# The normalization step of each layer norm: nine ScalarE instructions, or four two-scalar VectorE instructions

## The chip, the cores and the metric

The kernel runs on one core of a Trainium2 chip. The metric is the device time of one launch in microseconds (us). The core's engines each run their own queue of instructions in order: PE (TensorE, matmuls), DVE (VectorE), ACT (ScalarE), POOL (GpSimd) and SP (SyncE, which issues most DMAs). Weight loads of PE are shown apart, as PEld.

## The reference, cut to what matters

An input of 4 images of 64 x 64 positions with 128 channels passes through four layers, all in float32.

```python
def _ln(x, w, b):
    mu = x.mean(-1, keepdims=True)
    var = ((x - mu) ** 2).mean(-1, keepdims=True)
    return (x - mu) * jax.lax.rsqrt(var + 1e-05) * w + b
...
# layer 0, a state space layer
xz = _ln(input, ln1_w, ln1_b) @ in_proj_w            # ln1
...                                                  # 3x3 depthwise conv, silu
def step(h, t):                                      # 4 directions, 256 channels x 16 states, 4096 steps
    h = jnp.exp(d_t[..., None] * A) * h + (d_t * x_t)[..., None] * B_t[:, :, None, :]
    return (h, jnp.einsum('bkdn,bkn->bkd', h, C_t))
...
x = input + y @ out_proj_w
h2 = jax.nn.gelu(_ln(x, ln2_w, ln2_b) @ fc1_w + fc1_b, approximate=False) @ fc2_w + fc2_b   # ln2
x = x + h2
# layer 1: attention over all 4096 positions, layer 2: a block of convolutions
# layer 3: 7x7 neighborhood attention, then an MLP
x = x + _neighborhood_attention(_layernorm(x, norm1_g, norm1_b), ...)   # norm1
y = jax.nn.gelu(_layernorm(x, norm2_g, norm2_b) @ fc1_w + fc1_b, approximate=False)   # norm2
return x + y @ fc2_w + fc2_b
```

Four layer norms over 128 channels matter here: ln1, ln2, norm1 and norm2. Each is done in chunks of 512 positions, 8 chunks to an image, so there are 4 x 4 x 8 = 128 calls.

## The kernel before, in words

**The stages.** For each image: `scan_inputs` (ln1, projections, the 3x3 convolution, the step sizes), `selective_scan` (the recurrence), `scan_output` (gating, output projection, ln2, MLP), `layer1`, `layer2`, `layer3_attention` (norm1) and `layer3_mlp` (norm2, MLP). The scan is the long work of DVE and POOL, and the other stages are laid beside it. While image 0 is scanned, `scan_inputs` of images 1 to 3 is done. While image n is scanned, the rest of image n - 1 is done, with the last MLP of image n - 2 joined to its `scan_output`. When the last scan is over, the rest of image 3 follows alone, with the MLP of image 2 at its start and that of image 3 at its end.

**The scan.** It works in 512 units for each image; a unit is two tiles of 128 rows x 512 steps. POOL multiplies `dB` for both (L501, 128x1024, four buffers). For each of the two, ACT makes `dA = exp(...)` into one of three PSUM buffers (L507), and DVE runs the recurrence (L509) with `dA` from PSUM and `dB` from SBUF. For most units DVE writes the result over `dA` and then multiplies it by the row of C into `hc` (L514). For 5 of 16 units in image 0, and 7 of 16 in the others, DVE writes the states to `hc` and POOL multiplies (L522); that instruction is issued two units later. ACT copies the last state (L516, L518). PE sums the products (L555).

**A layer norm** (`layernorm_T`) takes four groups of 128 positions. DVE makes mean and variance (L188, L190), ACT makes `rstd = exp(-0.5 ln(var + eps))` (L174, L175). The step that is changed writes `xn`, of which there is one buffer. PE transposes the four groups into PSUM (L201), and ACT applies the weight and the bias (L202). In what follows "a call" is one such chunk.

**The order.** No order is written out by hand. The kernel names priorities (the scan has a late one, so that the other stages go first where they can), and a scheduler, which works with its own estimates of how long each instruction takes, lays out each engine's queue before the kernel runs. Dependencies between engines become semaphores. Groups of Gelu and of Silu are held together on ACT, because they need another table than Exp and Ln; each such group loads a table before and after it (L96, L226, L359).

A second path, `everything_again`, is in the program for inputs whose values are out of bounds. It also calls `layernorm_T`, but it isn't run with these inputs.

Other lines that are spoken of: L598 and L601 scale and set up weights on DVE at the start of each `scan_output`. L889, on POOL, takes a power in the setup of layer 2, and L890 to L894 are DVE instructions beside it. L1100, L1101, L1151 and L1198 to L1205 are small DVE instructions that check bounds or set up a bias table. L328 is POOL's product `du` in `scan_inputs`. L623 and L648 are gating and sum on DVE in `scan_output`.

Of the kernel before, what the change touches and what calls it, by code (L numbers as in the profile page):

```python
# [28 lines left out]
F32 = mybir.dt.float32  # L29
AF = mybir.ActivationFunctionType  # L30
ALU = mybir.AluOpType
# [140 lines left out]
def rstd_of(nc, K, out, var):  # L172

    nc.scalar.activation(out, var, AF.Ln, bias=K.eps)  # L174
    nc.scalar.activation(out, out, AF.Exp, scale=-0.5)  # L175


def layernorm_T(tc, K, pool, psum, x, w, b, out):


    nc = tc.nc
    stats = pool.tile([128, 4, 6], F32, name="ln_stats", bufs=2)
    mv = pool.tile([128, 4, 2], F32, name="ln_mv", bufs=2)
    rstd = pool.tile([128, 4], F32, name="ln_rstd", bufs=2)
    less = pool.tile([128, 4], F32, name="ln_less", bufs=2)
    shift = pool.tile([128, 4], F32, name="ln_shift", bufs=2)
    for t in range(4):
        nc.vector.bn_stats(stats[:, t, :], x[:, t, :])  # L188
    for t in range(4):
        nc.vector.bn_aggr(mv[:, t, :], stats[:, t, :])  # L190
    rstd_of(nc, K, rstd, mv[:, :, 1])
    nc.scalar.activation(less, rstd, AF.Copy, scale=-1.0)
    for t in range(4):
        nc.scalar.activation(shift[:, t : t + 1], mv[:, t, 0:1], AF.Copy, scale=less[:, t : t + 1])
    xn = pool.tile([128, 4, 128], F32, name="ln_xn", bufs=1)
    pt = psum.tile([128, 4, 128], F32, name="ps")
    for t in range(4):
        nc.scalar.activation(  # L198
            xn[:, t, :], x[:, t, :], AF.Identity, bias=shift[:, t : t + 1], scale=rstd[:, t : t + 1]
        )  # L200
        nc.tensor.transpose(pt[:, t, :], xn[:, t, :], K.ident)  # L201
    nc.scalar.activation(out, pt.rearrange("p t c -> p (t c)"), AF.Identity, bias=b, scale=w)  # L202
# [74 lines left out]
def scan_inputs(tc, K, A, D, img):  # L277
# [5 lines left out]
    with ExitStack() as ctx:  # L283
# [50 lines left out]
        for c in range(NCH + 1):  # L334
            acts = []
            if c < NCH:
                xt = pool.tile([128, 4, 128], F32, name="x")
                nc.sync.dma_start(xt, token_tiles(A["x"][img], c))
                xnT = pool.tile([128, LC], F32, name="xnT")
                layernorm_T(tc, K, pool, psum, xt, ln_w, ln_b, xnT)  # L340
                band = pool.tile([128, ND, RC + 2, W], F32, name="band", bufs=3)
                bands[c] = band
                for d in range(ND):
                    ps = psum.tile([128, LC], F32, name="ps")
                    nc.tensor.matmul(ps, in_proj[:, d * 128 : (d + 1) * 128], xnT, start=True, stop=True)
                    rows = ps.rearrange("p (h w) -> p h w", w=W)
                    nc.scalar.copy(band[:, d, 1 : RC + 1, :], rows)
                    if c > 0:
                        nc.scalar.copy(bands[c - 1][:, d, RC + 1, :], rows[:, 0, :])
                        nc.scalar.copy(band[:, d, 0, :], bands[c - 1][:, d, RC, :])  # L350
                sz = pool.tile([128, ND, LC], F32, name="sz")
                for d in range(ND):
                    ps = psum.tile([128, LC], F32, name="ps")
                    mm = nc.tensor.matmul(
                        ps, in_proj[:, DI + d * 128 : DI + (d + 1) * 128], xnT, start=True, stop=True
                    )
                    if d == 0:
                        together.open(mm)
                    acts.append(lambda d=d, ps=ps, sz=sz: nc.scalar.activation(sz[:, d, :], ps, AF.Silu))  # L359
# [221 lines left out]
def scan_output(tc, K, A, D, img, xT, last, scan_over=None):  # L581
# [6 lines left out]
    with ExitStack() as ctx:  # L588
# [17 lines left out]
        def chunk(c, psum=psum, together=together):  # L606
# [44 lines left out]
            yield  # L651
            xnT = pool.tile([128, LC], F32, name="xnT")
            layernorm_T(tc, K, pool, psum, x, ln_w, ln_b, xnT)
            yield
            po = yield from mlp(tc, K, P, pool, psum, together, xnT, x)
# [582 lines left out]
def layer3_attention(tc, K, A, D, img, wide):  # L1238
# [7 lines left out]
    with ExitStack() as ctx:  # L1246
# [33 lines left out]
        def make_chunk(c):  # L1280
            x = pool.tile([128, 4, 128], F32, name="x", bufs=6 if wide else 2)
            nc.sync.dma_start(x, token_tiles(D.x4[img], c))
            xs[c] = x
            xn = pool.tile([128, LC], F32, name="xnT", bufs=1)
            layernorm_T(tc, K, pool, made_in, x, n_w, n_b, xn)
            ps = fresh((128, 2, LC))
            for i in range(2):
                nc.tensor.matmul(ps[:, i, :], qkv[:, span(i, C)], xn, start=True, stop=True)
            qs[c] = pool.tile([128, LC], F32, name="q")
            nc.scalar.activation(qs[c], ps[:, 0, :], AF.Identity, bias=qb, scale=HD**-0.5)  # L1290
            ks[c] = pool.tile([128, LC], F32, name="k", bufs=3)
            nc.scalar.activation(ks[c], ps[:, 1, :], AF.Identity, bias=qkv_b[:, 1:2])
            ps = fresh((128, 4, 128))
            for t in range(4):
                nc.tensor.matmul(ps[:, t, :], xn[:, span(t, 128)], qkv[:, 2 * C :], start=True, stop=True)
            vs[c] = pool.tile([128, 4, 128], F32, name="v", bufs=3)
            nc.scalar.copy(vs[c], ps)
# [477 lines left out]
```

## Time and profile before

| | |
|---|---|
| Runs of the kernel | 8887.86, 8895.40, 8905.56 us; median 8895.4 us |
| The profiled execution | 8915.71 us, span 8914.0 us, mean granted PE clock 0.866 |
| Busy in the span | PE 80%, DVE 80%, ACT 63%, POOL 79%, PEld 30% |
| Instructions | PE 30116, DVE 8483, ACT 11581, POOL 3064 |
| DMA | 1581.91 MB, mean 177 GB/s |

A page of the profile lists busy time by engine, the span in 40 slices, the DMA queues, the chain of work that ended last, and groups of instructions. A group's row reads: line, engine, operation, output <- inputs, shapes, count | busy us and mean ns of one | idle time of the engine just before these instructions, and what ended it. The timeline gives start and duration in us of single instructions.

The layer norm's other instructions on DVE are short: L188 had a median of 278 ns, L190 of 158 ns. L198 had a median of 482 ns, L194 of 280 ns and L192 of 205 ns. Short instructions that follow each other on ACT overlap a little, so that busy time is less than count times mean.

### The profile page before, as it was taken

How to read it: one execution, taken by the hardware profiler on the slowest of the kernel's cores; microseconds unless marked ns; L12 is line 12 of the kernel's file. 1: busy time of each engine (PE TensorE's matmuls, PEld its weight loads, DVE VectorE, ACT ScalarE, POOL GpSimd, SP SyncE). 2: the span in 40 equal slices, each digit the busy share in tenths (PEclk: the TensorE clock that was granted, in tenths of full speed). 3: DMA queues.
4: the chain of work that ended last, by engine and by line, in shares of the span. 5: the costliest groups of instructions: out<-in, count | busy, mean ns of one | idle time of the engine just before them, and what ended most of it. 6: DMA issues, size and time to landing. Idle time of an engine off the chain costs nothing. (4 is left out here: it accounts for less than half of the span.)

```text
span 8914.0 us, 101143 instructions
## 1 busy us (share of the span) xinstructions
PE 7120.9 (80%) x30116; PEld 2708.4 (30%) x30116; DVE 7132.4 (80%) x8483; ACT 5640.4 (63%) x11581; POOL 7043.5 (79%) x3064
## 2 busy tenths in 40 slices
PE   5844858687689898887798888777888987888987
PEld 2211313132332233333332233233322332353333
DVE  3888878888899999998899989998999989513433
ACT  5646667676566666666766666667766666454355
POOL 5987899989799998998899989988899989500000
PEclk8856968687799998898899998888899988899989
DMA  5777677777555556665555556565445566320020
GB/s 172 248 236 240 224 249 240 262 242 265 180 175 166 172 174 211 192 215 190 165 174 168 176 183 213 194 213 178 165 165 174 180 204 198 107 69 4 7 80 29
DMA packets 864124, 1581.91 MB, mean 177 GB/s; under 512 B 219701, under 2 KB 344780, under 8 KB 859213
## 3 DMA queue, kind: packets, MB, share of 16 engines
q1 hardware_dynamic: 733261, 1399.17, 47.9%
q10 hardware_dynamic: 130304, 176.19, 5.6%
q8 instruction: 241, 3.95, 0.2%
q14 instruction: 318, 2.61, 0.1%
HBM read 1280.47 MB, written 283.59 MB: 175 GB/s over the span
## 5 line engine op out<-in xcount | busy, mean ns | idle before, releaser
L501 POOL TENSOR_TENSOR dB<-du,b_rows 128x1024 f32<-128x1024 f32 x2048 | 4817.8, 2389 | 553.6 <-DVE hc L509 137.0
L507 ACT ACTIVATE dA<-dt,w_A_log 128x512 f32<-128x512 f32 x4096 | 2785.3, 690 | 487.8 <-DVE hc L509 210.9
L509 DVE TENSOR_TENSOR_SCAN dA<-dA,state,dB 128x512 f32<-128x512 f32 x2128 | 2634.8, 1275 | 242.6 <-POOL dB L501 129.4
L522 POOL TENSOR_TENSOR hc<-hc,c_rows 128x1024 f32<-128x1024 f32 x832 | 1988.6, 2390 | 34.7 <-issue 16.1
L509 DVE TENSOR_TENSOR_SCAN hc<-dA,state,dB 128x512 f32<-128x512 f32 x1456 | 1805.4, 1270 | 218.8 <-ACT dA L507 134.6
L514 DVE TENSOR_TENSOR hc<-dA,c_rows 128x512 f32<-128x512 f32 x2432 | 1568.2, 679 | 76.1 <-PE py L555 61.1
L555 PE MATMUL py<-hc,pick 128*32 128x512 f32 x8192 | 1244.2, 685 | 380.2 <-POOL hc L522 307.3
L516 ACT COPY state<-dA 128x1 f32<-128x1 f32 x2128 | 327.6, 158 | 1348.3 <-DVE hc L514 1339.5
L845 PE MATMUL pa<-e,l_v 128*128 128x512 f32 x2048 | 1069.7, 654 | 21.1 <-ACT e L801 19.9
L797 PE MATMUL pair<-l_g,l_f 32*128 32x512 f32 x2048 | 527.1, 663 | 181.1 <-ACT e L801 139.2
L801 ACT ACTIVATE e<-pair 128x1024 f32<-128x1024 f32 (+1 forms) x448 | 508.2, 1134 | 226.9 <-PE pair L797 219.1
L845 PEld LDWEIGHTS pa<-e,l_v 128*128 128x128 f32 x2048 | 375.5, 200 | 673.9 <-issue 618.1
L555 PEld LDWEIGHTS py<-hc,pick 128*32 128x32 f32 x8192 | 211.5, 116 | 1147.5 <-issue 466.4
L247 PE MATMUL ps<-band,w_conv_diag 128*128 128x504 f32 (+3 forms) x1152 | 502.1, 595 | 7.7 <-ACT delta L397 6.6
L1303 PE MATMUL pair<-table,ident 128*128 128x512 f32 x768 | 398.9, 644 | 97.2 <-ACT e L1313 76.5
L509 DVE TENSOR_TENSOR_SCAN dA<-dA,dB 128x512 f32<-128x512 f32 x304 | 356.8, 1215 | 75.6 <-POOL dB L501 62.3
L328 POOL TENSOR_TENSOR du<-delta,xc 128x1024 f32<-128x1024 f32 x128 | 334.7, 2623 | 57.2 <-ACT delta L397 48.9
L1313 ACT ACTIVATE e<-pair 128x1024 f32<-128x1024 f32 (+1 forms) x224 | 254.7, 1137 | 186.5 <-PE pair L1307 185.9
L201 PE MATMUL ps<-ident,ln_xn 128*128 128x128 f32 x512 | 136.5, 362 | 291.0 <-ACT ln_xn L198 221.6
L219 PE MATMUL ps<-xnT,w_fc_w 128*128 128x512 f32 x512 | 271.6, 666 | 71.6 <-ACT xnT L202 44.6
L247 PEld LDWEIGHTS ps<-band,w_conv_diag 128*128 128x128 f32 x1152 | 221.3, 194 | 288.7 <-issue 259.3
L797 PEld LDWEIGHTS pair<-l_g,l_f 32*128 32x128 f32 x2048 | 139.0, 188 | 537.6 <-ACT e L801 275.0
(274 smaller groups left out, 8551.0 us busy)
## 6 DMA issues: line engine op xcount, KB each, us to landing
b_rows<-bc_dram SPq DMA_DIRECT2D x1024, 256.0 KB
c_rows<-bc_dram SPq DMA_DIRECT2D x1024, 256.0 KB
dt<-delta_dram SPq DMA_DIRECT2D x512, 512.0 KB
du<-du_dram SPq DMA_DIRECT2D x512, 512.0 KB
delta_dram<-delta ACTq DMA_DIRECT2D x128, 512.0 KB
du_dram<-du SPq DMA_DIRECT2D x128, 512.0 KB
table<-biasT_dram SPq DMA_DIRECT2D x72, 512.0 KB
y_first_dram<-y_sum ACTq DMA_DIRECT2D x128, 256.0 KB
```

Source lines behind the costliest of these rows:

```text
L247: mm = nc.tensor.matmul(out[:, r0 - row0 : r1 - row0, c0:c1], lhsT((dy + 1) * 3 + dx + 1), src[:, r0 + dy : r1 + dy, c0 + dx : c1 + dx], s ...
L328: nc.gpsimd.tensor_mul(du.rearrange("p d (a b) -> p d a b", b=H), deltas[b].rearrange("p d (a b) -> p d a b", b=H), tk,)
L501: nc.gpsimd.tensor_mul(dB, dus[pp], mid(bt, 2))
L507: nc.scalar.activation(dA, dts[pp][:, g, :], AF.Exp, scale=S.A[:, k, j, pr, g : g + 1])
L509: nc.vector.tensor_tensor_scan(hg[:, order], dA[:, order], dB[:, g, order], 0.0 if i == 0 else state[:, j, pr, g : g + 1], ALU.mult, ALU.add,)
L514: mm = nc.vector.tensor_mul(hc[:, g, :], dA, ct)
L522: made.append(nc.gpsimd.tensor_mul(hc, hc, mid(ct, 2)))
L555: mm = nc.tensor.matmul(py[0][32 * q : 32 * q + 32, :], S.pick, hcs[q // 2][:, q % 2, :], start=(k == 1 and j == 0), stop=(j == NJS - 1),)
L797: nc.tensor.matmul(ps[:, u, :], f[quad, t // 4, span(t % 4, 128)], g[quad, c, :], start=True, stop=True)
L801: made = nc.scalar.activation(e, ps, AF.Exp)
L845: nc.tensor.matmul(pa, v[:, 8 * q + t, :], es[q], start=(t == 0 and q == 0), stop=(t == 7 and q == 3),)
L1303: nc.tensor.matmul(ps[:, u, :], K.ident, t[:, u, :], start=True, stop=False)
```

## The change

The two small tiles `less` and `shift` go. Before, ACT made `less = -rstd` (one instruction), `shift = mean * less` (four) and `xn = x * rstd + shift` (four). Now DVE makes `xn = (x - mean) * rstd` in four instructions, which take the mean and rstd of each position as two column scalars.

```diff
-    less = pool.tile([128, 4], F32, name="ln_less", bufs=2)
-    shift = pool.tile([128, 4], F32, name="ln_shift", bufs=2)
...
     rstd_of(nc, K, rstd, mv[:, :, 1])
-    nc.scalar.activation(less, rstd, AF.Copy, scale=-1.0)
-    for t in range(4):
-        nc.scalar.activation(shift[:, t : t + 1], mv[:, t, 0:1], AF.Copy, scale=less[:, t : t + 1])
     xn = pool.tile([128, 4, 128], F32, name="ln_xn", bufs=1)
     pt = psum.tile([128, 4, 128], F32, name="ps")
     for t in range(4):
-        nc.scalar.activation(
-            xn[:, t, :], x[:, t, :], AF.Identity, bias=shift[:, t : t + 1], scale=rstd[:, t : t + 1]
+        nc.vector.tensor_scalar(
+            xn[:, t, :], x[:, t, :], mv[:, t, 0:1], rstd[:, t : t + 1], ALU.subtract, ALU.mult
         )
         nc.tensor.transpose(pt[:, t, :], xn[:, t, :], K.ident)
     nc.scalar.activation(out, pt.rearrange("p t c -> p (t c)"), AF.Identity, bias=b, scale=w)
```

## The prediction

> **What bounds the kernel now.** I read the slices of the page first, then busy time by stretch, then single instructions in the timeline.
>
> The slices (busy tenths of each engine in 40 slices of 223 us) show two parts. Up to slice 34, about 7680 us, VectorE and POOL are both nearly full; after that POOL has nothing to do. ScalarE is never full.
>
> ```profile
> DVE  3888878888899999998899989998999989513433
> ACT  5646667676566666666766666667766666454355
> POOL 5987899989799998998899989988899989500000
> ```
>
> The same by stretch (from:to, length, then busy time and count of PE, weight loads, DVE, ACT, POOL): the layer norms before the scan (780 to 960 is one of three such stretches), the first layer norm of layer 3 beside the scan (3400 to 3920), those ahead of the two MLPs beside the scan (4050 to 4420).
>
> ```profile
> 780.00:960.00 180.00, 134.38 (x424) 51.28 (x424) 148.66 (x209) 135.56 (x338) 144.17 (x63) 0.87 0.64 217
> 3400.00:3920.00 520.00, 416.94 (x2268) 156.59 (x2272) 495.24 (x573) 343.96 (x741) 513.98 (x223) 0.87 0.65 209
> 4050.00:4420.00 370.00, 288.40 (x1173) 145.15 (x1174) 316.40 (x463) 279.64 (x647) 300.32 (x130) 0.84 0.55 183
> ```
>
> In the second POOL is busy 514 of 520 us: it is the bound, DVE (0.95) only a little behind. In the others POOL (0.80, 0.81) and DVE (0.83, 0.86) both have gaps, made by waits on each other, on ScalarE and on PE.
>
> The chain of waits breaks off in the scan, so it is of use only for the end: from 7820 us on it is mostly PE, with ScalarE's layer norm steps between.
>
> **What goes.** Groups by form (count, then busy us and mean ns):
>
> ```profile
> L198 ACT ACTIVATE ln_xn<-x,ln_shift,ln_rstd 128x128 f32<-128x128 f32 x512 | 214.4, 485 | 0.0
> L194 ACT ACTIVATE ln_shift<-ln_mv,ln_less 128x1 f32<-128x1 f32 x512 | 108.1, 284 | 1.6
> L192 ACT ACTIVATE ln_less<-ln_rstd 128x4 f32<-128x4 f32 x128 | 24.4, 201 | 2.2 <-ACT ln_rstd L175 0.5 <-ACT state L516 0.2
> L598 DVE TENSOR_SCALAR out_proj_b<-w_out_proj_w,w_onorm_b 128x128 f32<-128x128 f32 x8 | 4.9, 653 | 4.5 <-DMA w_out_proj_w<-in_L_conv_out_proj_w 4.5
> ```
>
> There are 128 layer norms. ScalarE loses 214.4 + 108.1 + 24.4 = 346.9 us, 2.71 us for each. By the starts of L192, 8 of them lie before 600 us, 24 between 780 and 1950 (image 0's scan), 23 in the layer 3 stretches and 40 in the MLP stretches beside the later scans, and 33 after 7680.
>
> **What comes.** Four DVE instructions each, 128x128 f32 from SBUF to SBUF, with two column scalars. The nearest row is L598: same shape, one column. L894 with two constants took 226 ns, L648 with a PSUM source 345; between these the cost is bounded. Two undisturbed L598 took 0.48 us together (4034.01 below), so I take 0.24 each, 0.96 a call, 123 us in all. In the order of the changed kernel the four stand in a row in nearly every case, among the scan's instructions.
>
> **The wait that comes with them.** L598 has a mean of 653 ns though its median is 284. The timeline says why (start, duration, engine, instruction). POOL:
>
> ```profile
> 2253.14 4.63 POOL L501 TENSOR_TENSOR dB<-du,b_rows 128x1024 f32<-128x1024 f32 x2
> 2257.73 2.33 POOL L522 TENSOR_TENSOR hc<-hc,c_rows 128x1024 f32<-128x1024 f32 x1
> 2260.03 4.64 POOL L501 TENSOR_TENSOR dB<-du,b_rows 128x1024 f32<-128x1024 f32 x2
> 2264.63 2.34 POOL L522 TENSOR_TENSOR hc<-hc,c_rows 128x1024 f32<-128x1024 f32 x1
> ...
> 5935.68 2.35 POOL L501 TENSOR_TENSOR dB<-du,b_rows 128x1024 f32<-128x1024 f32 x1 [2.67 <-DMA sz<-sz_dram]
> ```
>
> and DVE in the same stretches:
>
> ```profile
> 2253.60 13.52 DVE L601 TENSOR_TENSOR center<-center,ident 128x128 f32<-128x128 f32 x1
> 4034.01 0.48 DVE L598 TENSOR_SCALAR out_proj_b<-w_out_proj_w,w_onorm_b 128x128 f32<-128x128 f32 x2 [2.13 <-DMA w_out_proj_w<-in_L_conv_out_proj_w]
> 5936.63 1.67 DVE L598 TENSOR_SCALAR out_proj_b<-w_out_proj_w,w_onorm_b 128x128 f32<-128x128 f32 x2
> ```
>
> L601 lasts 13.52 us and ends at 2267.12, 0.15 us after the sixth POOL instruction in an unbroken row (2264.63 + 2.34 = 2266.97). With POOL idle (4031.6) it took 0.28. L598 at 5936.63 took 1.48 us for its first, which ends 0.08 us after POOL's L501; its second took 0.27. So a DVE instruction that reads two SBUF tensors, or is a 128x128 SBUF-to-SBUF tensor_scalar, stands still while POOL works, and is let in only when POOL pauses. The scan's own DVE instructions, which have one source in PSUM, and bn_stats (254 to 302 ns in all 512) show nothing of this. The new instruction has L598's shape, so I take it to wait too.
>
> [...]
>
> How long would each wait be? At each start of L192 beside the scan I followed POOL's queue and asked what it could still do if DVE stood still: a dB for at most four units (bufs=4), and a product only of a unit already scanned. Summed: 86 us for the 24 calls before 1950, 132 us for the 23 of layer 3, 58 us for the 40 ahead of MLPs: 276 us for 87 calls, 3.2 each. Bounds for one: 0 (not held up) and 13.52.
>
> Behind the standing instruction are queued the scans (L509) and products (L514). For them wait ScalarE's L516 and L507 (three dA buffers), then POOL, which finds no free dB. What this costs goes by stretch.
>
> - **Start (8 calls): 0.** POOL's L889, a power, lasts 20.82 us (20.74 to 41.56). If it shuts DVE out, the first eight instructions end near 44 instead of 29; it may not, for two tiny DVE instructions (L891, L892) passed beside it in 0.15 us. The first xnT (L202) waits for the load of ln_w until 48.11 anyway. Without that cover it would be some 15 us.
> - **Layer 3 (23 calls): +80.** POOL is the bound, so only POOL's idle time counts. DVE gets in when POOL has run out of free dB. POOL then idles through the four instructions (0.96) and two scans of 1.27 (2.55) until a dB comes free: 3.5 us a call. DVE cannot make the wait good before the next call (75 us × 0.05 spare = 3.7 us against 132/23 = 5.7 + 0.96), so it repeats. Bounds: 0, and the full 6.7 × 23 = 154.
> - **Before the scan's end of image 0 (24 calls): +42.** POOL has a share of 0.80 to 0.88 here, so some idle time is free. I take half of 3.5. Bounds: −31 (DVE's 10.4 us of waits for dA in the first stretch, times three, all gone) and 86 + 23 = 109.
> - **Ahead of MLPs (40 calls): 0.** Lost: up to 1.45 + 0.96 = 2.4 us a call, 96 in all. Gained: ScalarE is free of 2.71 us a call, and DVE waits there for ScalarE's dA 46.7, 35.2 and 13.1 us in the three stretches, 95 in all. I take half of each. Bounds −95 and +96.
> - **After the scan (33 calls): −20.** POOL is idle, no wait. On the chain of waits, L192, L194 and L198 stand for 22 us (four pieces of 1.7 to 2.8 in the MLP pair, 9.0 together; nine of 0.7 to 1.8 around layer 3, 9.8; 3.5 in the last MLP). Little comes back, since DVE is idle. Bounds −45 and 0.
> - **A new dependence: 0.** DVE now waits for ScalarE's rstd. Nearest rows: L623 waited 71.7 us for ScalarE in 64, 1.1 each; L648, which follows an rstd too, 5.1 us in 128. Such a wait runs into the same POOL idle time. Bounds: 0 and 87 × 1.1 = 96.
>
> The kernel's order is made by a scheduler, and POOL's and SP's instructions move by a few places too. I put nothing on this.
>
> **Sum.** 0 + 80 + 42 + 0 − 20 = +102 us. The profiled execution took 8915.7 us (span 8914.0), 20.3 above the median of 8895.4. So 8895.4 + 102 = 8997.
>
> **Rivals.**
> 1. *Faster: ScalarE's relief wins.* The standing falls into gaps that DVE has anyway (DVE idles 718 us of the 7010 in the stretches from 600 to 7660), and the MLP stretches gain: −95 × 0.6 there, −20 at the end, +20 in layer 3: 8895 − 57 = 8838. For it: DVE and POOL are both under 0.9 in 64 of the 87 calls' stretches. Against it: POOL's 0.99 in layer 3.
> 2. *The wait does not come at all*, because the form with two columns, unlike L598, runs beside POOL. Then DVE's 87 × 0.96 = 84 us hide in its gaps but for about 25, relief is as above: −57 − 20 − 31 × 0.5 + 25 = 8828. Against it: L598 and L1199 (7.28 us), both tensor_scalar.
> 3. *Far slower: every wait counts in full*, since DVE stands and nothing takes it up: 276 + 84 − 20 = +340, 9235. It decides if waits are as long as the ten I found on DVE instructions with two SBUF operands or of tensor_scalar (1.3 to 13.5 us, mean 4.6), and POOL's lead doesn't shrink. Against it: POOL works on while DVE stands.
>
> **How the numbers follow.** Forecast 0.63, rival 1 0.22, rival 2 0.06, rival 3 0.09. About 0.2% (18 us) is what a measurement of this kernel can tell from no change. The forecast's low end and rival 1's high end give 0.11 within it. Slower: 0.56 of the forecast and 0.09 of rival 3, 0.65; faster 0.24. All bounds together reach from 8724 to 9350; ends at once are unlikely. From 8850 to 9170 leaves out rival 3's upper part (0.08) and the lower parts of rivals 1 and 2 (0.12).
>
> **What would show it.** The new DVE row should have a minimum near 0.24 to 0.3 us, and beside the scan about one in four of 1 to 10 us, ending just after a POOL instruction; after the scan none. Its busy time should be near 350 to 400 us, against 123 unhindered. ScalarE should be 347 us shorter. In 3400 to 4000 POOL's share should fall below 0.97, with dB waiting for scans; after the scan the rest should be some 20 us shorter. I am wrong if the row's longest is under 0.5 us, if POOL's share in layer 3 stays, or if the MLP stretches shorten by more than 40 us.

## The result, and the profile after

| | before | after |
|---|---|---|
| Runs beside each other, median | 8891.63 us (8886.56 to 8905.56, 4 runs) | 9035.4 us (9025.69 to 9045.01, 4 runs) |
| Ratio | | 1.0155, 95% interval 1.0143 to 1.0167 |
| Profiled execution, span | 8914.0 us | 9035.4 us |
| DVE, ACT, POOL busy in the span | 80%, 63%, 79% | 84%, 59%, 78% |
| Mean granted PE clock | 0.866 | 0.855 |

The change costs 138 us by the ratio (127 to 149 by the interval; the two medians lie 144 apart); +102 was forecast. Lines of after are five below those of before from the dB product on: the new instruction is L193, dB is L496, the recurrence L504, the products L509 (DVE) and L517 (POOL).

The slices of after, each 226 us long (DVE, ACT and POOL busy, in tenths):

```profile
DVE  4888888797899999999999989999999899953433
ACT  4645656666466665565666655556666665554344
POOL 5887898978889997997799979987899899930000
```

POOL's work now ends in the 36th digit (a 3) and not in the 35th; the digits ahead of it differ by a tenth here and there, so the loss has to be read from stretches. The three stretches that the prediction showed, at their new times (from:to, length, then busy time and count of PE, weight loads, DVE, ACT, POOL; granted clock, DMA share, GB/s):

```profile
780.00:970.00 190.00, 137.28 (x408) 51.49 (x408) 167.64 (x230) 112.88 (x259) 139.60 (x61) 0.79 0.58 197
3480.00:4000.00 520.00, 399.30 (x2152) 151.24 (x2152) 502.15 (x563) 300.26 (x617) 480.62 (x208) 0.83 0.58 191
4110.00:4480.00 370.00, 280.85 (x1142) 145.12 (x1141) 343.47 (x511) 224.69 (x446) 273.04 (x118) 0.82 0.52 169
```

In layer 3 POOL is busy 480.6 of 520 us (0.92), where it was 514 (0.99): what was the bound now has gaps, while DVE, with 502, looks fuller. That fullness is not work. It is the new instruction, whose group by form is

```profile
L193 DVE TENSOR_SCALAR ln_xn<-x,ln_mv,ln_rstd 128x128 f32<-128x128 f32 x512 | 464.3, 966 | 86.8 <-PE ps L196 66.1 <-ACT ln_rstd L175 20.7
```

a mean of 966 ns. By minimum, median and longest (with first and last start), for all 512, and then for those that start after the scan:

```profile
L193 DVE TENSOR_SCALAR ln_xn<-x,ln_mv,ln_rstd x512: 302/340/7567, 23.5 to 9005.5; 128x128 f32<-128x128 f32 x171
```

```profile
L193 DVE TENSOR_SCALAR ln_xn<-x,ln_mv,ln_rstd x124: 334/341/348, 7991.1 to 9005.5; 128x128 f32<-128x128 f32 x124
```

Unhindered one took 0.34 us, and after the scan, where POOL is idle, none of the 124 took more than 0.348. Four in a row overlapped: each started 0.26 us after the one ahead of it, and a whole call took 1.11 us.

```profile
8017.22 1.11 DVE L193 TENSOR_SCALAR ln_xn<-x,ln_mv,ln_rstd 128x128 f32<-128x128 f32 x4 [3.84 <-PE ps L196]
```

Beside the scan 142 of the 512 took over 0.5 us; what they took above 0.34 adds up to 322 us, and all 142 ended 79 to 90 ns after the end of a POOL instruction.

One layer norm in layer 3, in the timeline (start, duration, engine, instruction). POOL first, then DVE:

```profile
3659.66 2.38 POOL L517 TENSOR_TENSOR hc<-hc,c_rows 128x1024 f32<-128x1024 f32 x1
3661.96 4.67 POOL L496 TENSOR_TENSOR dB<-du,b_rows 128x1024 f32<-128x1024 f32 x2
3666.55 2.38 POOL L517 TENSOR_TENSOR hc<-hc,c_rows 128x1024 f32<-128x1024 f32 x1
```

```profile
3661.45 8.34 DVE L193 TENSOR_SCALAR ln_xn<-x,ln_mv,ln_rstd 128x128 f32<-128x128 f32 x4
```

The four stand for 8.34 us. POOL goes through an unbroken row until 3668.93, and the first of the four ends just after that, at about 3669.0 (it is the one of 7.57 us); the other three then take 0.33 each. This is the picture of L601 in the profile before. Ahead of it, in `scan_inputs`, the picture is another one:

```profile
258.60 2.35 POOL L517 TENSOR_TENSOR hc<-hc,c_rows 128x1024 f32<-128x1024 f32 x1
260.91 2.36 POOL L496 TENSOR_TENSOR dB<-du,b_rows 128x1024 f32<-128x1024 f32 x1
263.22 4.64 POOL L323 TENSOR_TENSOR du<-delta,xc 128x1024 f32<-128x1024 f32 x2
```

```profile
260.44 7.50 DVE L193 TENSOR_SCALAR ln_xn<-x,ln_mv,ln_rstd 128x128 f32<-128x128 f32 x4
```

Here the four took 0.595, 2.391, 2.378 and 2.374 us: each of the last three waited for one POOL instruction, was let in, and the next waited again, though POOL's row is as unbroken. And beside one POOL instruction there was no wait at all: L884, the power (L889 before). Two calls ran in the middle of it, unhindered. POOL, then DVE:

```profile
20.66 20.82 POOL L884 TENSOR_TENSOR w_last<-w_last,mhalf 128x128 f32<-128x128 f32 x1
```

```profile
23.54 1.12 DVE L193 TENSOR_SCALAR ln_xn<-x,ln_mv,ln_rstd 128x128 f32<-128x128 f32 x4 [0.17 <-ACT ln_rstd L175]
25.30 1.11 DVE L193 TENSOR_SCALAR ln_xn<-x,ln_mv,ln_rstd 128x128 f32<-128x128 f32 x4 [0.64 <-PE ps L196]
```

The POOL instruction whose end let a held one in was a product of 128x1024 in all 142 cases (L496 71 times, L517 48, L323 23).

What the waits come to, by stage, beside what the prediction counted (87 calls by starts in the trace of before; here 88 and the first 8):

| stage | calls | instructions over 0.5 us | waited, us | longest, us | counted before |
|---|---|---|---|---|---|
| first 8 calls | 8 | 13 | 22.7 | 2.42 | not counted |
| ln1 beside scan 0 | 24 | 49 | 91.8 | 6.84 | 86 |
| layer 3 (norm1) | 24 | 27 | 116.6 | 7.57 | 132 |
| ahead of the MLPs | 40 | 51 | 87.9 | 2.45 | 58 |

Two more instructions, 3.0 us of waiting together, belong to a call of image 2's last MLP that starts at 7920.6, before the scan's end. The waits are there in about the counted size. What became of them is seen at two points of the trace, the start of the last scan instruction and that of the last sum of image 2's attention (L1342 before, L1337 after), on which the rest of image 2's layer 3 ends:

| | last scan instruction | last sum of image 2's attention | later of the two, against before | span, against before |
|---|---|---|---|---|
| before | 7699.9 | 7815.7 | 0 | 0 |
| after | 7985.3 | 7889.3 | +169.6 | +121.4 |

Before, the scan was over 116 us ahead of that attention. In those 116 us DVE and POOL had next to nothing to do:

```profile
7700.00:7816.00 116.00, 95.90 (x558) 40.28 (x556) 7.25 (x17) 28.39 (x40) 0.95 (x1) 0.90 0.15 47
```

In after it is the other way round. From 7889 to 7985 the scan runs on with little beside it, DVE is full and PE is half idle:

```profile
7889.00:7985.00 96.00, 46.73 (x180) 19.12 (x180) 94.93 (x112) 39.34 (x77) 83.38 (x37) 0.68 0.53 171
```

So the scan slipped by 285 us and the other stages by 74, and which of the two comes last has changed.

### The profile page after: what moved, and what is told of

It is laid out like the page before. It is cut to its first block, busy times and chain, and to the rows that moved or that the text cites. A ratio compares the mean times of both kernels' runs of the same rounds, so it can differ in the third digit from the quotient of the medians.

```text
span 9035.4 us, 100375 instructions
## 1 busy us (share of the span) xinstructions
PE 7148.6 (79%) x30116; PEld 2729.3 (30%) x30116; DVE 7579.7 (84%) x8995; ACT 5340.8 (59%) x10429; POOL 7048.3 (78%) x3064
## 5 line engine op out<-in xcount | busy, mean ns | idle before, releaser
L496 POOL TENSOR_TENSOR dB<-du,b_rows 128x1024 f32<-128x1024 f32 x2048 | 4806.2, 2374 | 823.4 <-DVE dA L504 195.8
L504 DVE TENSOR_TENSOR_SCAN dA<-dA,state,dB 128x512 f32<-128x512 f32 x2128 | 2627.3, 1271 | 216.4 <-POOL dB L496 109.4
L517 POOL TENSOR_TENSOR hc<-hc,c_rows 128x1024 f32<-128x1024 f32 x832 | 1976.0, 2375 | 52.4 <-issue 20.2
L504 DVE TENSOR_TENSOR_SCAN hc<-dA,state,dB 128x512 f32<-128x512 f32 x1456 | 1800.0, 1267 | 143.9 <-ACT dA L502 81.1
L509 DVE TENSOR_TENSOR hc<-dA,c_rows 128x512 f32<-128x512 f32 x2432 | 1562.0, 675 | 99.0 <-PE py L550 88.0
L193 DVE TENSOR_SCALAR ln_xn<-x,ln_mv,ln_rstd 128x128 f32<-128x128 f32 x512 | 464.3, 966 | 86.8 <-PE ps L196 66.1
L504 DVE TENSOR_TENSOR_SCAN dA<-dA,dB 128x512 f32<-128x512 f32 x304 | 356.6, 1212 | 69.4 <-POOL dB L496 50.8
L323 POOL TENSOR_TENSOR du<-delta,xc 128x1024 f32<-128x1024 f32 x128 | 332.8, 2607 | 49.8 <-ACT delta L392 43.6
```

Source lines behind the costliest of these rows:

```text
L193: nc.vector.tensor_scalar(xn[:, t, :], x[:, t, :], mv[:, t, 0:1], rstd[:, t : t + 1], ALU.subtract, ALU.mult)
L496: nc.gpsimd.tensor_mul(dB, dus[pp], mid(bt, 2))
L504: nc.vector.tensor_tensor_scan(hg[:, order], dA[:, order], dB[:, g, order], 0.0 if i == 0 else state[:, j, pr, g : g + 1], ALU.mult, ALU.add,)
L509: mm = nc.vector.tensor_mul(hc[:, g, :], dA, ct)
L517: made.append(nc.gpsimd.tensor_mul(hc, hc, mid(ct, 2)))
```

## The experiments

The intervals are at 95%, against runs of the kernel before on the same chip. Differences in us are the ratio less one, times the median of before beside it (8898 to 8903 us).

**Is it the second operand's place?** The same work in one DVE instruction of another form, with rstd as a full operand in PSUM rather than a column in SBUF. ACT writes rstd into a corner of the PSUM tile that the transposes fill afterwards, so the four transposes come after all four instructions.

```diff
-    rstd_of(nc, K, rstd, mv[:, :, 1])
+    nc.scalar.activation(rstd, mv[:, :, 1], AF.Ln, bias=K.eps)
+    nc.scalar.activation(pt[:, 3, 0:4], rstd, AF.Exp, scale=-0.5)
...
-        nc.vector.tensor_scalar(
-            xn[:, t, :], x[:, t, :], mv[:, t, 0:1], rstd[:, t : t + 1], ALU.subtract, ALU.mult
-        )
+        nc.vector.scalar_tensor_tensor(
+            xn[:, t, :], x[:, t, :], mv[:, t, 0:1], bc(pt[:, 3, t : t + 1], [128, 128]), ALU.subtract, ALU.mult
+        )
```

> The four DVE instructions become scalar_tensor_tensor with rstd read from PSUM, (x - mean) * rstd with one SBUF source, so that they are like the DVE rows that never stood still (0.33 to 0.36 us each). ScalarE is relieved as in the change, DVE has as much or more to do. If standing still beside POOL is the cause: no instruction over 0.5 us, and the time returns to before or under it, 8830 to 8900 us. If the cause is DVE's added work or the new order of instructions: 9000 to 9060 us.

Measured (e1): 8797.47 us, ratio 0.9883 (0.9866 to 0.9899), -104 us, faster than the range expected. The instruction, its group by form, and layer 3 (same columns as above):

```profile
L194 DVE SCALAR_TENSOR_TENSOR ln_xn<-x,ln_mv,ps x512: 302/341/349, 23.9 to 8769.9; 128x128 f32<-128x128 f32 x171
```

```profile
L194 DVE SCALAR_TENSOR_TENSOR ln_xn<-x,ln_mv,ps 128x128 f32<-128x128 f32 x512 | 142.2, 340 | 175.7 <-ACT ps L192 173.9 <-PE ps L198 1.5
```

```profile
3400.00:3920.00 520.00, 428.18 (x2421) 160.66 (x2420) 499.04 (x579) 326.64 (x666) 520.00 (x225) 0.88 0.63 206
```

The same 0.34 us as an unhindered L193, and not one of 512 above 0.349. POOL is busy all 520 us of layer 3. The form alone could be what differs, so the next kernel keeps the form and puts rstd back into SBUF.

```diff
-    nc.scalar.activation(pt[:, 3, 0:4], rstd, AF.Exp, scale=-0.5)
+    nc.scalar.activation(rstd, rstd, AF.Exp, scale=-0.5)
...
-            xn[:, t, :], x[:, t, :], mv[:, t, 0:1], bc(pt[:, 3, t : t + 1], [128, 128]), ALU.subtract, ALU.mult
+            xn[:, t, :], x[:, t, :], mv[:, t, 0:1], bc(rstd[:, t : t + 1], [128, 128]), ALU.subtract, ALU.mult
```

> The same scalar_tensor_tensor instructions as in the kernel with rstd in PSUM, with rstd in SBUF: two SBUF sources, nothing else. If what counts is whether an instruction stands still beside POOL: waits of 1 to 10 us come back and the time is 9000 to 9060 us. If that kernel's gain came from another thing (its transposes set after all four, the order): within 20 us of 8797.

Measured (e5): 9060.85 us, ratio 1.0179 (1.0162 to 1.0196), +159 us.

```profile
L194 DVE SCALAR_TENSOR_TENSOR ln_xn<-x,ln_mv,ln_rstd x512: 315/344/8677, 23.7 to 9026.3; 128x128 f32<-128x128 f32 x171
```

152 of them took over 0.5 us, 338 us in waits. Where four small columns lie, SBUF or PSUM, is worth 263 us of the kernel's time. With the same work on DVE and the same relief of ACT, these 338 us of waits move the last scan instruction by 290 (from 7718.8 to 8008.6).

**The wait alone, without the work.** The kernel before, with one added product of 128x2 for each layer norm, whose result nobody reads; and beside it one with a reduction of the same small size that reads one SBUF tensor.

```diff
     rstd_of(nc, K, rstd, mv[:, :, 1])
+    tiny = pool.tile([128, 2], F32, name="ln_tiny", bufs=2)
+    nc.vector.tensor_mul(tiny, rstd[:, 0:2], mv[:, 0, :])
```

> The kernel before, with one added DVE instruction per layer norm, a product of two SBUF columns of 128x2 that nobody reads (0.15 us unhindered, 19 us in all 128). If the standing beside POOL is the cause, its mean is about 3 us beside the scan and the kernel is 60 to 150 us slower than before. If not, it is within 20 us of before.

```diff
+    nc.vector.tensor_reduce(tiny, rstd.rearrange("p (a b) -> p a b", b=2), AX.X, ALU.max)
```

> The kernel before, with one added DVE instruction per layer norm at the same place as in the last one, but with one SBUF source (a maximum over pairs, 128x2 from 128x4, not read by anybody). It too waits for rstd and takes a place in DVE's queue. If standing beside POOL is the cause: never over 0.3 us, and the time within 20 us of before. If the wait for ScalarE's rstd or the place in the queue is the cause, it costs as much as the two-column product.

Measured: with the product (e2) 8992.84 us, ratio 1.0107 (1.009 to 1.0124), +95 us; with the reduction (e3) 8897.39 us, 0.9999 (0.9989 to 1.0009). First the product, then the reduction:

```profile
L193 DVE TENSOR_TENSOR ln_tiny<-ln_rstd,ln_mv x128: 116/161/9976, 24.0 to 8956.0; 128x2 f32<-128x2 f32 x128
```

```profile
L193 DVE TENSOR_REDUCE ln_tiny<-ln_rstd x128: 110/150/159, 24.5 to 8873.0; 128x2 f32<-128x4 f32 x128
```

128 instructions of 0.16 us, 20 us of work in all, cost 95 us of the kernel's time, because 47 of them were held for 147 us together. Those that read one SBUF tensor cost nothing that can be measured. Of the 78 us by which the last scan instruction came later, nearly all arose in the three layer 3 stretches (+27, +19 and +23 us, by the start of the same scan instruction in both kernels).

**After the scan alone.** Each call of `layernorm_T` is given a name, and a flag says whether the call is laid beside a scan; DVE's form is used only where a rule says so, else the code of before.

```diff
-def layernorm_T(tc, K, pool, psum, x, w, b, out):
+ON_DVE = lambda name, beside: not beside
+def layernorm_T(tc, K, pool, psum, x, w, b, out, name):
+    on_dve = ON_DVE(name, K.beside)
```

> DVE makes xn only in the layer norms of image 3's rest after the scan (and those of image 2's last MLP, 32 calls), ScalarE in all others as before. By the forecast's term for the end: 20 us faster than before, 8865 to 8885. If a shorter ScalarE does not matter at the end: 8892 within 8 us.

Measured (e4): 8869.64 us, ratio 0.9966 (0.9954 to 0.9979), -30 us, within the range of the forecast's term.

```profile
L202 DVE TENSOR_SCALAR ln_xn<-x,ln_mv,ln_rstd x128: 332/342/350, 7814.4 to 8834.9; 128x128 f32<-128x128 f32 x128
```

No wait. In its profiled execution the stretch from the end of image 2's attention to the end is 28 us shorter, 1070 us against 1098 before (and 1094 to 1100 in e6, e7 and e8 below, which change nothing there). Its span is 49 us shorter than that of before, but the other 21 us lie ahead of that point, where the code is that of before, and so is the order of instructions on DVE, ACT and POOL (on PE a few matmuls change places). They look like the spread of executions, for the profiled one of before was 12 to 24 us above its medians. The 28 us fit the -30 of the runs.

**Each stage beside the scan alone**, by the rule:

```diff
-ON_DVE = lambda name, beside: not beside
+ON_DVE = lambda name, beside: beside and name == "ln1"
```

> DVE makes xn as in the change, but only in the 32 calls of the first layer norm; ScalarE makes it in the others. By the forecast's term +42 us, 8925 to 8955. By the trace of the changed kernel, in which the rest of image 0 began 53 us later: 8930 to 8960. If waits there fall into gaps: 8895 within 20.

Measured (e6): 8985.5 us, ratio 1.0091 (1.0074 to 1.0107), +81 us, more than any of the three expectations. 62 instructions were held, for 114 us; scan 0 ended 116 us later.

```diff
+ON_DVE = lambda name, beside: beside and name == "norm1"
```

> DVE makes xn as in the change, but only in the first layer norm of layer 3 beside the scan (24 calls). By the forecast's term +80, by the kernel with the added product +67: 8950 to 8985. If only the other stretches cost: 8895 within 20.

Measured (e7): 8922.49 us, ratio 1.0025 (1.0015 to 1.0035), +22 us, a quarter of what I had put on it, and between the two expectations. The waits are there, 30 of them for 104 us, the longest longer than any in after:

```profile
L202 DVE TENSOR_SCALAR ln_xn<-x,ln_mv,ln_rstd x96: 302/335/10214, 3419.3 to 7717.7; 128x128 f32<-128x128 f32 x96
```

and the last scan instruction came 108 us later. But the attention of image 2 was done only 11 us later, and the end followed the attention. So a slip of the scan is not yet a slip of the end.

```diff
+ON_DVE = lambda name, beside: beside and name in ("ln2", "norm2")
```

> DVE makes xn as in the change, but only ahead of the MLPs beside the scan (40 calls). The forecast's term is 0: 8895 within 20. If the two to three waits of 2.4 us in each call count in full: 40 x 4 us, 9030 to 9060. If ScalarE's relief wins: under 8875.

Measured (e8): 8904.94 us, ratio 1.0005 (0.9995 to 1.0014), +4 us, no difference that can be told from none. 49 instructions held for 83 us; last scan instruction 70 us later, the attention 2 us earlier.

**Do two slips that cost little alone cost more together?** If the end waits for the later of the scan and the attention, layer 3 and MLP stages together must use up the 116 us by which the scan was ahead; if each stage has its own price, they add up to 22 + 4 = 26 us.

```diff
+ON_DVE = lambda name, beside: beside and name != "ln1"
```

> DVE makes xn as in the change in the 64 calls of layer 3 and ahead of the MLPs beside the scan, ScalarE in the rest. Each group alone moved the end of the last scan by 108 and 70 us, but the end of the kernel by 24 and 7 only: after the last scan the attention of image 2 still ran for 116 us in the kernel before, and hid the shift. If that slack is why the parts do not add up, the two together use it up: 108 + 70 - 116 = 62, 8950 to 8975. If the parts simply add: 8925 to 8935.

Measured (e9): 8973.92 us, ratio 1.0085 (1.0068 to 1.0101), +76 us. The last scan instruction is 188.5 us late, 72.7 past where the attention ended before, and the attention itself is 2 us early. The price is not a sum over stages.

**The best version.** e1's instruction beside the scans, ACT's code of before after them:

```diff
+ON_DVE = lambda name, beside: beside
...
+    if on_dve:
+        nc.scalar.activation(rstd, mv[:, :, 1], AF.Ln, bias=K.eps)
+        nc.scalar.activation(pt[:, 3, 0:4], rstd, AF.Exp, scale=-0.5)
+        for t in range(4):
+            nc.vector.scalar_tensor_tensor(
+                xn[:, t, :], x[:, t, :], mv[:, t, 0:1], bc(pt[:, 3, t : t + 1], [128, 128]), ALU.subtract, ALU.mult
+            )
```

> The instruction with rstd in PSUM, which never stood still, in the layer norms up to the end of the last scan alone; after it ScalarE makes xn as before (32 calls). If the relief of ScalarE beside the scan is worth most of the 106 us which that kernel gained: 8810 to 8840. If most of it lies after the scan: 8870 to 8900.

Measured (e10): 8784.43 us, ratio 0.9872 (0.9856 to 0.9889), -114 us, faster than either expectation. This and e1 (0.9866 to 0.9899) can't be told apart, so the relief beside the scan gives the whole of e1's gain. The scan itself ends 12 us later than before; the attention of image 2 ends 171 us earlier, so that less is left for the time after the scan.

The two points of the trace in all of these, from one profiled execution each (before had 8915.7 us, 12 to 24 above its medians, so the last column lies about that much under the differences of medians):

| | last scan instruction | last sum of image 2's attention | later of the two, against before | span, against before |
|---|---|---|---|---|
| before | 7699.9 | **7815.7** | 0 | 0 |
| after | **7985.3** | 7889.3 | +169.6 | +121.4 |
| e1, PSUM, all calls | **7718.8** | 7648.3 | -96.9 | -119.5 |
| e2, tiny product | 7777.8 | **7892.5** | +76.8 | +74.7 |
| e3, tiny reduction | 7699.2 | **7812.3** | -3.4 | -8.0 |
| e4, after the scan only | 7681.0 | **7794.6** | -21.1 | -49.1 |
| e5, SBUF, all calls | **8008.6** | 7939.2 | +192.9 | +142.1 |
| e6, ln1 only | 7777.1 | **7884.4** | +68.7 | +70.2 |
| e7, norm1 only | 7808.2 | **7827.0** | +11.3 | +6.9 |
| e8, MLPs only | 7769.8 | **7813.3** | -2.4 | -3.8 |
| e9, norm1 and MLPs | **7888.4** | 7813.6 | +72.7 | +55.1 |
| e10, PSUM, beside only | **7711.5** | 7644.3 | -104.2 | -134.9 |

The later of the two (bold) gives the span to within 5 us in every kernel where the attention is last and nothing, or the tiny instruction alone, is changed behind it (e2, e3, e6, e7, e8). Where the scan is last, or where the instructions behind it are changed too, the span is 18 to 51 us better than that.

## Why the prediction was right, and where it wasn't

**The mechanism was right.** DVE instructions that read two SBUF tensors, and the tensor_scalar with columns, stood still while POOL did its products of 128x1024. The trace of after has it in 142 of 512 instructions (up to 7.57 us), e5 against e1 has it for one form with only the operand's place changed (152 of 512, up to 8.68 us, against none over 0.349), and e2 against e3 has it for an instruction of 0.16 us (47 of 128, up to 9.98 us with two SBUF tensors, against none over 0.159 with one). Whether a tensor_scalar would pass with its columns in PSUM was not tried. The granted PE clock is lower in after (0.855 against 0.866). No run sets it apart, but it leaves little to explain: the waits by which e5 and e1 differ come to 338 us, the scan's end to 290, and in the long stretch behind the scan the clock was 0.93 in after and 0.92 before.

The signs named beforehand came: waits of up to 7.57 us, 142 of the 388 instructions that start ahead of the scan's end (37%, where one in four was forecast), none after the scan, POOL at 0.92 in layer 3, dB waiting for scans:

```profile
POOL dB L496 <- DVE dA L504: 23.7, 8, 3.4
```

(us in all, times, longest, from 3480 to 4100: 3.0 us each, where 3.5 was worked out.) Two signs missed: DVE's new row was busy 464 us, not 350 to 400, and ACT's busy time fell by 300 us (from 5640.4 to 5340.8), not by 347. The prediction had added up three rows whose instructions overlap with others of ACT; the relief is 2.3 us a call, not 2.71. Rival 2, no wait at all, fell with that. Rival 3, all waits in full at the end, fell too: at +138 the end took over less than half of the waits, though the scan took most (below).

A held instruction was not always let in at the end of the POOL instruction that was under way: the wait of 7.57 us goes through three boundaries between POOL instructions. And a POOL instruction did not always block: beside the power of 20.82 us, which takes two SBUF tensors, eight of L193 were not held (1.11 and 1.12 us for each four), nor eight in e5 and four in e2.

**Unhindered time.** I took 0.24 us for each, from two L598 in 0.48 together. In the same measure it is 0.28, four in 1.11; all 512 are 142 us (e1's row) in place of 123, and e1 shows that DVE had room for it.

**Counting the waits.** Counted 276 us for 87 calls, measured 296 in the same stages, close in ln1 and in layer 3. But the prediction's step "is let in only when POOL pauses" holds in the main for layer 3 alone: there 22 of the 27 waits ended where POOL's row broke off, while 27 of the 49 in ln1 and 17 of the 51 ahead of the MLPs ended between two POOL instructions less than 0.1 us apart. I had taken one wait for each call. In ln1 and ahead of the MLPs there were often two or more, up to three of 2.4 us and a shorter one. In ln1 a single wait was shorter than counted (91.8/49 = 1.9 us against 86/24 = 3.6), so that the two errors offset each other; ahead of MLPs it was longer (87.9/51 = 1.7 against 58/40 = 1.45), and the sum came out half as large again.

**Start, 0.** The question whether the power shuts DVE out is answered: it didn't. But the last four of the eight calls come at 131 to 268 us, when scan 0 is under way, and had 23 us of waits, for which the prediction had no term. E6 can't tell what these cost from its other 24 calls.

**"Before the scan's end of image 0: +42"** was half of what it is: +81 (e6). The step that failed is "I take half of 3.5", on the ground that POOL has free time there. In e6 scan 0 ended 116 us later, with 114 us of waits and 36 us of new work on DVE (32 calls of 1.11): the gaps of POOL and DVE and ACT's relief together took up little of it. (In e2, whose waits there come to 32 us and whose work is next to nothing, scan 0 ended only 9 us later, so half is no safe figure either way.) Here the other stages slip as well, since the rest of image 0 comes behind `scan_inputs` and has to wait for it (its gating starts 54 us later in e6), and so the slip reaches the end.

**"Layer 3: +80"** and **"Ahead of MLPs: 0"** are the terms whose step was wrong in kind. On the scan both were too small: +108 and +70 us at its end, for 104 and 83 us of waits and 27 and 44 us of new work. At the end of the kernel they are +22 and +4 alone and +76 together, where +80 and 0 were forecast. The 0 ahead of the MLPs was met by luck: ACT's relief did not balance the waits there, the scan slipped and its lead hid it. The step that failed is the sum itself, which took a slip of the scan for a slip of the end. The profile of before had shown what stands between: the last scan instruction starts at 7699.9 and image 2's attention runs on until 7815.7, and what is left of image 3 isn't done until both are over. I had read this stretch as "after the scan", with POOL idle, and not asked who would be waited for if the scan came later.

**"After the scan: -20"**: e4 shows -30, of which 28 us are seen behind the attention. In after, the time behind the later of the two points shrank by 48 us (169.6 - 121.4); e9, with nothing changed there, shows 18 of these (72.7 - 55.1), which leaves 30.

**"A new dependence: 0"** was near enough. The group's row has 20.7 us of waiting for rstd in 512 instructions (4.2 of them ahead of the scan's end), and 66.1 us for PE's transposes, because xn has one buffer; the prediction had not named the second one. In e1, where nothing stands still, DVE waits longer for rstd: 173.9 us, 62.5 of them ahead of the scan's end.

**The sum** was therefore right in part by luck. It had the scan's end at +122 and what follows at -20; the profiled executions show +285 and -164. The scan took up most of the waits, where the forecast let many of them fall into gaps or be balanced; and of what follows, 116 us vanished because the scan's lead hid them, and 48 because that stretch got shorter. The two errors had opposite signs.

**Rival 1** had a true half. Taking 2.3 us a call off ACT seems worth more than the 67 us that rival 2, without the wait, put on it: e10 gains 114 with 96 of the 128 calls, and image 2's attention, which shares ACT with the scan, ends 171 us earlier. That the same relief lies inside after is seen in e7 and e8, where the attention keeps its time (+11, -2) while the scan slips, and in e2, which relieves nothing, where both slip (+78, +77). That it is ACT's queue by which the attention gains is argued from this; no run took the work off ACT without putting some on DVE.

**What stays open.** At the boundaries between POOL instructions that follow each other within 0.1 us, the waiting L193 (those over 0.5 us) was let in 27 times of 31 in ln1 and 17 of 18 ahead of the MLPs, but 5 of 40 in layer 3. E5 has the same picture (28 of 32, 22 of 22, 6 of 40). What decides it, and why the power on POOL held nothing, wasn't tried.

## What to carry to other kernels

Before work is moved to DVE beside a busy POOL, look at where its operands lie: here instructions with two operands in SBUF (up to 8.68 us, and up to 9.98 us for one of 0.16 us) and a 128x128 tensor_scalar with columns (up to 7.57 us in after, 10.21 in e7) were held, some of them for several POOL instructions of 2.4 us, and one operand in PSUM took that away (302 to 349 ns against up to 8677). When stages run beside each other, find the two or three points for which the end waits, and follow each one through the change; here a slip of the one that was early cost little until its lead of 116 us was used up (+4 us for a slip of 70, +22 for one of 108), and the prices of stages didn't add (76 us for the two together). An engine at 63% busy is no proof that relief of it is worth little: here 114 us came with it, though that they came through its queue was argued and not shown.

## What the runs showed of the hardware that was not expected

A 128x2 product of two SBUF tensors on DVE, 0.16 us of work, was held for 9.98 us. All 142 held instructions of after ended 79 to 90 ns after the end of a POOL instruction (in e5 146 to 154 ns), but seldom after the first one in layer 3 (let in at 5 of 40 boundaries) and nearly always in ln1 (27 of 31). Beside POOL's power of 20.82 us none was held. A scalar_tensor_tensor of 128x128 lasted the same 0.34 us as a tensor_scalar with two columns (medians 341 and 340 ns), and with its second operand in PSUM it wasn't held in any of 512 instructions.
